# A fifth tile bank and a timetable for block work in layer 1, with shared banks, two projection banks and stepwise finishing in layer 2, of a two-layer relational graph convolution

## The chip, the cores and the metric

The kernel runs on one core of one Trainium2 chip. The metric is the device time of one execution in microseconds. The median of three runs of the kernel before is 3691.99 us (3690.94 to 3702.55).

## The reference

There are N = 12500 nodes with C = 128 features, E = 200000 edges sorted by destination, and ten relations. The relation of an edge is the position of the largest of ten columns of its attributes. Two layers of relational convolution are followed by a residual and a layer norm:

```
def _rgcn_layer(x, src, dst, edge_type, w_rel, root, bias):
    seg  = dst * 10 + edge_type
    sums = segment_sum(x[src], seg, N * 10)
    cnt  = segment_sum(1, seg, N * 10)
    mean = (sums / max(cnt, 1)).reshape(N, 10, C)
    return einsum('nrd,rdo->no', mean, w_rel) + x @ root + bias
h   = relu(layer(x, ..., w_rel1, root1, b1))
out = layernorm(x + layer(h, ..., w_rel2, root2, b2))
```

## The kernel before

**Tiles and blocks.** Edges are worked on in 1563 tiles of 128. For each tile GpSimd (POOL in the profile) issues one indirect DMA, the gather (L833), that brings 128 source rows into a buffer `g`; VectorE (DVE) makes one-hot columns `oh` that say to which node and relation an edge goes, scaled by 1/count (L840); TensorE (PE) multiplies the two, which sums the edges of each node and relation into a PSUM bank; DVE adds the bank into accumulators in SBUF. Nodes are taken in blocks of 256, and a block is complete about every 32 tiles. All of it is in one program order that is written out by hand: three small queues of closures (`todo`, `between`, `jobs`) say at which tile a step is issued. Each engine takes its instructions in that order, so an instruction that waits holds up everything that is behind it on its engine.

**Layer 1.** The first 177 gathers bring rows of `x` (512 B); the other 1386 bring rows of a table XH that holds x and, for nodes that are done, h (1 KB), so that their product is at once a part of layer 2's sum. The products (L1077) go to four PSUM banks `zp`, two tiles in each; DVE adds them (L866) eight tiles later (BEHIND is 2 parts of 4 tiles). POOL may be 16 tiles ahead: four buffers of four tiles, each free when its last product is done.

When a block is complete, `finish(k, t)` issues: ten products with the relations' weights and one with root (L826, L828) into a `pf` bank, ScalarE (ACT) writes h, transposed, as `a` (L745); two transposes (L951) and an ACT copy `hb` (L958) give rows, which go to XH; and h times layer 2's ten relation weights goes out as the table YD. These are six matmuls per block (L934), four tiles apart, all into the one bank `yb`, and each is followed by an ACT copy `ys` (L940) and a store, which `kept_rows` issues when the next one comes. SD is the store of layer 2's sums so far, `cleared` zeroes accumulators on ACT (L795), and `turn` and `turned` transpose the next block's x (L996, L1003). The eight banks are: two `pf`, in which `projected`, the transposes, `turn` and the preparation of later tiles (`jobs`) take turns, one in which counts are kept, `yb`, and four `zp`.

**Layer 2.** Edges whose source had no h when layer 1 came by are gathered now from YD: 177 plain tiles (idxE) and then 678 "second" tiles (idxB), which are sorted by source class into bunches of 4, 2 or 1 tiles that accumulate into one window of 12 to 119 columns. Each bunch takes a bank of its own: three `zy`, and two more `zq` in the second part. POOL may be some 40 tiles ahead. `seen` brings in the blocks' stored sums SD: ten matmuls (L1521) into the one bank `alone`, every 12 tiles, with a DVE add (L1528) nine tiles after the first. `finish(j)` ends a block: two PE transposes (L1540), and at once behind them the layer norm on DVE and ACT (L773 to L783) and the store.

Of the kernel before, what the change touches and what calls it, by code (L numbers as in the profile page):

```python
# [9 lines left out]
F32 = mybir.dt.float32  # L10
# [3 lines left out]
ALU = mybir.AluOpType  # L14
# [6 lines left out]
P = 128  # L21
# [28 lines left out]
HB = 4  # L50
SPLIT = 64
LEAD = 40
LAST = 40
READY = 5
NEAR = 4
GAPW = 112
LOW = 1 << 13
# [11 lines left out]
def rgcn_resnorm_kernel(ctx: ExitStack, tc: tile.TileContext, x, src, dst, attr, w_rel1, root1, b1,  # L69
# [428 lines left out]

    def weights_in():
        for l, (wr, ro, bi) in enumerate(((w_rel1, root1, b1), (w_rel2, root2, b2))):  # L500
            t = const.tile([P, NREL, C], F32, name=f"w{l}")
# [238 lines left out]
    def shifted(po, k, l):  # L740

        n = block(k)[1]
        tail = {NBLK - 1: "e", NBLK - 2: "d"}.get(k, "")
        a = fin.tile([P, P if tail else 3 * P], F32, name="a" + tail)
        nc.scalar.activation(a[:, :n], po[:, :n], AF.Identity if l else AF.Relu, bias=bsb[l])  # L745
        return a
# [159 lines left out]
    def layer_1():  # L906
# [6 lines left out]
        def finish(k, t):  # L913
# [12 lines left out]
            assert not reused or t + 7 * u <= (starts[k] + RN - OFF - WN) // STEP  # L926

            fin_a[k] = shifted(po.pop(), k, 0)

            def projected_rows(b, h, r):  # L930
                kept_rows()
                m = min(HB, NREL - r) * C
                yb = yb_ if u else next_of("zp", fixed)
                nc.tensor.matmul(yb[:h, :m], fin_a[k][:, b * P:b * P + h], wsb[1][:, r:r + m // C, :], start=True, stop=True)  # L934
                unkept.append(lambda: projected_kept(yb, b, h, r))

# [51 lines left out]
            if k + 1 < NBLK - 1:  # L988
# [17 lines left out]
                todo.at(t + w * u, turn)  # L1006
                todo.at(t + (w + 1) * u, turned_kept)

        unkept = []

        def kept_rows(_=None):
# [407 lines left out]
    def layer_2():  # L1419
# [39 lines left out]
            return min(lo for lo, _ in r), max(hi for _, hi in r) + w  # L1459

        reaches = [reach(b) for b in bunches]
        cuts = list(range(0, N, BN)) + [a for a in range(0, N, P) if abs(a - edge) < BN]
        cuts = sorted(set(cuts))
        ranges.append([(a, b - a) for a, b in zip(cuts, cuts[1:] + [N])])
# [37 lines left out]

        def rows_in_turn(j):
            if j < NB2:
                xbs[finals[j]] = next_of("x", xs)
                rows_dma(xbs[finals[j]], x, finals[j], False)

        def seen_in(j):
# [6 lines left out]
        def seen(j, i):  # L1515
            k = heavy[j]
            n0, n, _ = block(k)
            po = alone[0]

            def one(r):  # L1520
                nc.tensor.matmul(po[:, :n], wsb[1][:, r, :], sds[k][:, r, :n], start=(r == 0), stop=(r == NREL - 1))  # L1521
                if r == NREL - 1:
                    sds.pop(k)
                    seen_in(j + 2)

            def added(_):
                assert k in begin[:begins]
                nc.vector.tensor_tensor(acc2[:, n0:n0 + n], acc2[:, n0:n0 + n], po[:, :n], op=ALU.add)  # L1528
                whole.add(k)
            for r in range(NREL):  # L1530
                between.at(i + 2 * r // 3, lambda _, r=r: one(r))
            between.at(i + 9, added)

        def finish(j):
            k = finals[j]
            n0, n, subs = block(k)
            assert k in whole or k not in heavy
            pr = ps_f.tile([P, 4, C], F32, name="pf")
            for b, h in subs:
                nc.tensor.transpose(pr[:h, b, :], acc2[:, n0 + b * P:n0 + b * P + h], ident)  # L1540
            normed(k, xbs.pop(k), pr, (next_of("v", vs), next_of("o", os_)))
            rows_in_turn(j + 3)

        rowP = comp.tile([1, 2 * CT], I32, name="rowP")
        for c in range(2):
# [20 lines left out]
        for p in range(-AH, NB + BE):  # L1566
            if p == plain - AH:
                assert wanted[0] in ready
                masking.close()
                ps_n = fast.enter_context(tc.tile_pool(name="ps_n", bufs=1, space=PSUM))  # L1570
                banks[:] = [next_of("zp", banks) for _ in banks] + [ps_n.tile([P, YB], F32, name=f"zq{j}") for j in range(2)]
# [16 lines left out]
            if p < NB:  # L1588
                second, t0, n, w = bunches[p]
                oh = ohs.pop(p)  # L1590
                zps[p] = zp = next_of("zp", banks)
# [12 lines left out]
                for j in range(n):  # L1604
                    g, at = gs.pop(j)
                    o = 0 if second else j * w
                    nc.tensor.matmul(zp[:, o:o + w], g[:, at * C:(at + 1) * C], oh[:, j * w:(j + 1) * w],  # L1607
                                     start=not second or j == 0, stop=not second or j == n - 1)
                    between.run(issued[p] + j + 1)
                i = issued[p + 1]  # L1610
# [7 lines left out]
            if opened is None and wanted[0] in ready:  # L1618
                opened = i
                for j in range(2):  # L1620
                    seen_in(j)
            for q in [q for q in sorted(zps) if q <= p - (1 if p >= NB - 4 else BE)]:
                second, t0, n, w = bunches[q]
                for j in range(1 if second else n):
                    t = t0 + j
                    if (second, t) not in offs:
# [10 lines left out]
                    nc.vector.tensor_tensor(s, s, zps[q][:, j * w:(j + 1) * w], op=ALU.add)  # L1637
                del zps[q]
            todo.run(i)
            summed_to = min(zps, default=min(p + 1, NB))  # L1640
            while ended < NB2 and done_at[finals[ended]] <= summed_to and (finals[ended] in whole or finals[ended] not in heavy):
                finish(ended)
# [172 lines left out]
```

## Time and profile before

| | us |
|---|---|
| median of three runs | 3691.99 (3690.94 to 3702.55) |
| the profiled execution | 3655.59, of which the span of instructions is 3653.8 |
| PE busy | 2254.1 (62%) |
| PE loading weights | 1859.4 (51%) |
| DVE busy | 1994.0 (55%) |
| ACT busy | 514.6 (14%) |
| POOL busy, 2418 gathers | 2294.6 (63%) |

No engine is busy for more than two thirds of the span. Four stages follow each other, and each is a run of gathers: 177 of x, 1386 of XH, 177 of YD by idxE, 678 of YD by idxB. A row of the groups of instructions reads: line, engine, operation, out<-in, count, then busy time and the mean ns of one, and behind the second bar how long the engine stood idle just before these instructions, and what ended most of it. In a row of the waits the three numbers are the total in us, how often, and the longest. "issue" is time in which the profile shows nothing that was waited for, "remote" is a release by something that the profile cannot name.

### The profile page before, as it was taken

Reading aid. Unit: us, or ns where it says so; the run is one execution under the profiler, and the core shown is the slowest. Engines: PE = TensorE matmul, PEld = TensorE weight load, DVE = VectorE, ACT = ScalarE, POOL = GpSimd, SP = SyncE. Lnnn points to the kernel's source line nnn. Section 1 sums busy time; section 2 is a strip of 40 time slices with the busy share of each in tenths; the row PEclk is TensorE's granted clock in tenths of the full one; section 3 lists DMA queues with packets and bytes.
Section 4 is the critical chain, followed back from the end, with each engine's and each line's share of the span. In section 5 each row is a group of like instructions: output and inputs, shape, how many; then the busy total and the mean of one; then the engine's idle time right before and its main releaser. Section 6 shows DMA issues by size and latency. Waiting matters only on the chain. (4 is left out here: it accounts for less than half of the span.)

```text
span 3653.8 us, 38569 instructions
## 1 busy us (share of the span) xinstructions
PE 2254.1 (62%) x11125; PEld 1859.4 (51%) x11125; DVE 1994.0 (55%) x6434; ACT 514.6 (14%) x799; POOL 2294.6 (63%) x2430
## 2 busy tenths in 40 slices
PE   1556677677676767676667667733556566566534
PEld 0445565565555555555555555623445555555433
DVE  4646576867565757565656565428654333233333
ACT  1111121212121212122212121100000000000000
POOL 5663666666666666666666666566566666666664
PEclk7677877878888888887888877855667777677655
DMA  4553656555555555555656555531144444444322
GB/s 122 154 170 96 189 155 192 153 186 165 172 172 169 172 177 176 171 182 158 191 159 194 158 161 157 146 98 51 46 117 135 143 137 140 136 151 135 97 61 51
DMA packets 376423, 529.31 MB, mean 145 GB/s; under 512 B 55904, under 2 KB 283707, under 8 KB 376204
## 3 DMA queue, kind: packets, MB, share of 16 engines
q0 software_dynamic: 99552, 249.45, 23.9%
q1 hardware_dynamic: 249209, 264.48, 22.4%
q10 hardware_dynamic: 27443, 12.82, 1.2%
q8 instruction: 93, 1.52, 0.2%
q14 instruction: 126, 1.03, 0.1%
HBM read 372.75 MB, written 160.19 MB: 146 GB/s over the span
## 5 line engine op out<-in xcount | busy, mean ns | idle before, releaser
L833 POOL DMA_INDIRECT g<-XH,idxE x1386 | 1314.1, 948 | 737.7 <-issue 364.8
L1077 PEld LDWEIGHTS zp<-oh,g 128*128 128x128 f32 x5898 | 901.7, 229 | 407.3 <-DVE cc L866 201.5
L1077 PE MATMUL zp<-oh,g 128*128 128x120 f32 x5898 | 943.1, 317 | 247.3 <-DVE cc L866 159.0
L866 DVE TENSOR_TENSOR cc<-cc,zp 128x240 f32 (+1 forms) x1563 | 607.1, 388 | 787.1 <-remote 353.0
L833 POOL DMA_INDIRECT g<-YD,idxB x678 | 642.6, 948 | 339.8 <-issue 185.9
L934 PE MATMUL yb<-w,a 128*128 128x512 f32 (+1 forms) x576 | 345.2, 689 | 346.0 <-ACT ys L940 183.1
L840 DVE TENSOR_SCALAR oh<-bank,keyE,wE 128x120 f32<-128x120 f32 x1563 | 517.7, 394 | 0.0
L1521 PE MATMUL alone<-cc,w 128*128 128x256 f32 (+2 forms) x920 | 339.4, 485 | 136.4 <-DVE cc L1528 72.8
L1607 PEld LDWEIGHTS zy<-oh,g 128*128 128x128 f32 x1168 | 245.9, 273 | 222.5 <-DVE cc L1637 155.1
L1607 PE MATMUL zy<-oh,g 128*128 128x12 f32 (+30 forms) x1168 | 237.2, 330 | 197.3 <-DVE cc L1637 148.2
L940 ACT ACTIVATE ys<-yb 128x512 f32<-128x512 f32 (+2 forms) x291 | 153.0, 526 | 1334.4 <-remote 553.7
L934 PEld LDWEIGHTS yb<-w,a 128*128 128x128 f32 x576 | 110.8, 240 | 379.1 <-ACT ys L940 203.6
L1521 PEld LDWEIGHTS alone<-cc,w 128*128 128x128 f32 x920 | 195.3, 247 | 158.3 <-DVE cc L1528 76.5
L826 PE MATMUL pf<-cc,w 128*128 128x256 f32 (+2 forms) x1040 | 248.4, 396 | 15.1 <-issue 9.2
L833 POOL DMA_INDIRECT g<-in_x_dram,idxE x177 | 167.8, 948 | 135.7 <-PE zp L1077 59.3
L833 POOL DMA_INDIRECT g<-YD,idxE x177 | 168.6, 953 | 111.1 <-issue 60.6
L826 PEld LDWEIGHTS pf<-cc,w 128*128 128x128 f32 x1040 | 205.7, 212 | 49.3 <-issue 19.8
L795 ACT ACTIVATE cc<-zero 128x1280 f32<-128x1280 f32 x170 | 214.6, 1262 | 0.0
L840 DVE TENSOR_SCALAR oh<-columns,keyB,wB 128x45 f32<-128x45 f32 (+35 forms) x678 | 177.0, 336 | 0.2 <-issue 0.2
L1637 DVE TENSOR_TENSOR cc<-cc,zy 128x12 f32 (+24 forms) x306 | 58.9, 192 | 177.8 <-remote 145.5
L1607 PEld LDWEIGHTS zq<-oh,g 128*128 128x128 f32 x542 | 113.2, 258 | 30.8 <-issue 18.4
L1528 DVE TENSOR_TENSOR cc<-cc,alone 128x256 f32<-128x256 f32 (+2 forms) x46 | 18.6, 405 | 199.3 <-remote 159.0
(265 smaller groups left out, 1563.5 us busy)
## 6 DMA issues: line engine op xcount, KB each, us to landing
SD<-cc SPq DMA_DIRECT2D x41, 1280.0 KB
cc<-SD SPq DMA_DIRECT2D x41, 1280.0 KB
YD<-ys SPq DMA_DIRECT2D x194, 256.0 KB
m<-in_edge_attr_dram SPq DMA_DIRECT2D x48, 672.0 KB
g<-XH,idxE POOLq DMA_INDIRECT x1386
YD<-ys SPq DMA_DIRECT2D x97, 128.0 KB
XH<-hb SPq DMA_DIRECT2D x44, 256.0 KB
g<-YD,idxB POOLq DMA_INDIRECT x678
```

Of the source, the lines that this page charges most:

```text
L795: nc.scalar.activation(cc[:, l, h * H:(h + 1) * H, o:o + n], zero[:, None, :n].to_broadcast([P, H, n]), AF.Copy)
L826: nc.tensor.matmul(po[:, :n], wsb[l][:, r, :], sums[:, r], start=(r == 0), stop=(w is None and r == NREL - 1))
L833: nc.gpsimd.indirect_dma_start(out=g[:, j * C:(j + n) * C], out_offset=None, in_=table, in_offset=bass.IndirectOffsetOnAxis(ap=idx, axis=0))
L840: nc.vector.tensor_scalar(oh[:, j * m:(j + 1) * m], cols[:, :m], keys[:, j:j + 1], weights[:, j:j + 1], op0=ALU.is_equal, op1=ALU.mult)
L866: nc.vector.tensor_tensor(s, s, z, op=ALU.add)
L934: nc.tensor.matmul(yb[:h, :m], fin_a[k][:, b * P:b * P + h], wsb[1][:, r:r + m // C, :], start=True, stop=True)
L940: nc.scalar.activation(ys[:h, :m], yb[:h, :m], AF.Copy)
L1077: nc.tensor.matmul(zp[:, o + l * KW:o + (l + 1) * KW], g[:, (slot[j] + l) * C:(slot[j] + l + 1) * C], oh[:, j * KW:(j + 1) * KW], start=Tr ...
L1521: nc.tensor.matmul(po[:, :n], wsb[1][:, r, :], sds[k][:, r, :n], start=(r == 0), stop=(r == NREL - 1))
L1528: nc.vector.tensor_tensor(acc2[:, n0:n0 + n], acc2[:, n0:n0 + n], po[:, :n], op=ALU.add)
L1607: nc.tensor.matmul(zp[:, o:o + w], g[:, at * C:(at + 1) * C], oh[:, j * w:(j + 1) * w], start=not second or j == 0, stop=not second or j = ...
L1637: nc.vector.tensor_tensor(s, s, zps[q][:, j * w:(j + 1) * w], op=ALU.add)
```

## The change

**Layer 1.** `zp` has five banks instead of four; `yb` is gone. For blocks up to K1 (44 of them) `finish` calls a new function `spread`, a timetable of steps at fixed numbers of tiles after the block is complete. The six projection matmuls become `unit`s that take a `pf` bank each, and each copy with its store (`unit_out`) is issued two tiles later, always ahead of the next unit. The identity is kept as an eleventh slot behind layer 2's weights, so that the last unit of a 128-row half (relations 8 and 9) is one matmul of 384 columns that also gives the transposed rows; the two transposes (L951) of a block are gone, and `hb` is copied in two halves. In the last blocks one `zp` bank takes the place of `yb`. READY goes from 5 to 7: rows of h may be read from XH eight tiles later than before, which moves seven gathers more to the second part of layer 2 (2425 in all).

**Layer 2.** Bunches share banks: a bank takes up to eight tiles or 512 columns. Second-part banks are three `zy` and one `zq`; `alone` has two banks in turn, and its add comes 20 tiles after the first matmul instead of nine. Sums are taken two banks behind. `finish` is three steps: transposes at least 8 tiles later, `measured` (sum, statistics, ACT's root) 9 tiles behind, `scaled` 4 behind that; in the last 32 tiles (RUSH) they follow at once.

On PE in the middle of layer 1, before: the matmuls into `yb` (L934) with products (L1077) between; DMASW is a gather's arrival, DVE the sum that empties a bank, Activation a copy on ACT.

```order
1593 L934 MATMUL yb<-w_391,a 128x512
1594 L1077 MATMUL zp_409<-oh_97,g_87 128x120 [waits DMASW4_49,DVE_49]
...
1599 L1077 MATMUL zp_410<-oh_97,g_87 128x120 [waits DMASW6_49,DVE_49]
...
1603 L934 MATMUL yb<-w_391,a 128x512 [waits Activation_49]
1604 L1077 MATMUL zp_407<-oh_98,g_88 128x120 [waits DMASW0_49,DVE_49]
...
1608 L1077 MATMUL zp_408<-oh_98,g_88 128x120 [waits DMASW2_49,DVE_49]
...
1612 L934 MATMUL yb<-w_391,a 128x256 [waits Activation_49]
```

The same place after the change, also on PE (L1033 are the units, L1145 the products, L1052 is `turn`, and L297 belongs to the jobs).

```order
1554 L1033 MATMUL pf<-w_113,a 128x384 [waits Activation_49]
1555 L1145 MATMUL zp_407<-oh_96,g_86 128x120 [waits DMASW2_49,DVE_49]
...
1559 L1033 MATMUL pf<-w_113,a 128x384
1560 L1145 MATMUL zp_408<-oh_97,g_87 128x120 [waits DMASW4_49,DVE_49]
...
1564 L297 MATMUL pf<-w_113,s_f 128x128 [waits DVE_49,PE_49,Activation_49]
1565 L1145 MATMUL zp_409<-oh_97,g_87 128x120 [waits DMASW6_49]
...
1573 L1052 MATMUL pf<-w_113,hb_6654 128x128 [waits DMAHW1_49,PE_49,Activation_49]
...
1583 L1033 MATMUL pf<-w_113,a 128x512 [waits Activation_49]
```

Every `yb` matmul waited for ACT's copy of the one before it; the units stand in a rotation of two banks with the other users of `pf`, and most of them (218 of 264 over the program) still carry a wait for ACT.

On PE in the second part of layer 2, before: each bunch goes to the next bank (`zy`, `zq`), and the first matmul of a block's ten waits for DVE's add of the block before.

```order
4712 L1607 MATMUL zq_17204<-oh_93,g_87 128x46 [waits DMASW3_49,DVE_49]
...
4719 L1499 MATMUL pf<-cc,root_393 128x256 [waits DMAHW2_49,Activation_49]
4720 L1607 MATMUL zy_15678<-oh_94,g_87 128x67 [waits DMASW7_49,DVE_49]
...
4722 L1607 MATMUL zy_15679<-oh_95,g_87 128x67 [waits DMASW1_49,DVE_49]
...
4724 L1607 MATMUL zy_15680<-oh_96,g_88 128x46 [waits DMASW3_49,DVE_49]
4725 L1521 MATMUL alone<-cc,w_391 128x256 [waits DMAHW3_49,DVE_49]
```

And after: three bunches (oh_96 to oh_98) share the bank zy_15855 before zy_15856 is taken.

```order
4685 L1737 MATMUL zy_15855<-oh_96,g_90 128x76 [waits DMASW1_49,DVE_49]
...
4687 L1624 MATMUL pf<-w_113,cc 128x128 [waits DVE_49]
...
4689 L1737 MATMUL zy_15855<-oh_97,g_91 128x76 [waits DMASW3_49,DVE_49]
4690 L1600 MATMUL alone_17337<-cc,w_113 128x256 [waits DMAHW6_49,DVE_49]
...
4694 L1737 MATMUL zy_15855<-oh_98,g_91 128x48 [waits DMASW5_49]
...
4702 L1737 MATMUL zy_15856<-oh_92,g_91 128x76 [waits DMASW1_49,DVE_49]
...
4711 L1600 MATMUL alone_17336<-cc,w_113 128x256 [waits DMAHW1_49,DVE_49]
```

The two `alone` banks alternate, so a block's matmuls wait for the add of the block before last; more of the tile products carry a wait for DVE than before (323 instead of 114 over layer 2).

On DVE in the second part, before: the add of `alone` (L1528) stands between the sums (L1637) and one-hots (L840) and waits for PE.

```order
5479 L1637 TENSOR_TENSOR cc<-cc,zq_17203 128x89 [waits DVE_49]
5480 L840 TENSOR_SCALAR oh_94<-columns,keyB,wB 128x93 x4
5481 L1528 TENSOR_TENSOR cc<-cc,alone 128x256 [waits PE_49]
...
5484 L1637 TENSOR_TENSOR cc<-cc,zq_17204 128x89 [waits DVE_49]
5485 L840 TENSOR_SCALAR oh_95<-columns,keyB,wB 128x98 x4
```

And after, where L1660 and L1662 are the step `scaled`, alone between other blocks' work, and the add (L1607) no longer carries a wait for PE of its own.

```order
5482 L1774 TENSOR_TENSOR cc<-cc,zy_15855 128x85 [waits DVE_49]
5483 L1660 RECIPROCAL rstd<-rstd 128x2 [waits Activation_49]
5484 L1662 TENSOR_SCALAR o_15872<-cc,mv,rstd 128x128 [waits DMAHW5_49,DVE_49]
...
5500 L1774 TENSOR_TENSOR cc<-cc,zy_15856 128x89
...
5504 L842 TENSOR_SCALAR oh_97<-columns,keyB,wB 128x98 x4
5505 L1607 TENSOR_TENSOR cc<-cc,alone_17337 128x256
```

An instruction ahead of it on DVE has waited for a later product already, so the add has none left to wait for.

The diff, cut to its core:

```diff
+RUSH = 32
-READY = 5
+READY = 7
-    ident = const.tile([P, P], F32, name="ident")
+    w1_ident = const.tile([P, NREL + 1, C], F32, name="w1")
+    ident = w1_ident[:, NREL, :]
...
@@ layer_1, finish(k, t)
+            if u and k <= K1:
+                spread(k, t, both, reused)
+                return
+            if not spare:
+                fixed[:] = [next_of("zp", fixed) for _ in fixed]
+                turn_of_["zp"] = 0
+                spare.append(fixed.pop(0))
...
-                yb = yb_ if u else next_of("zp", fixed)
+                yb = spare[0] if u else next_of("zp", fixed)
...
+        def spread(k, t, both, reused):
+            def unit(b, r):
+                a = fin_a[k][:, b * P:(b + 1) * P]
+                end = r + HB if r + HB < NREL else NREL + 1
+                held[b, r] = yb = ps_f.tile([P, YB], F32, name="pf")
+                nc.tensor.matmul(yb[:, :(end - r) * C], a, w1_ident[:, r:end, :], start=True, stop=True)
+            def unit_out(b, r):
+                yb = held.pop((b, r))
+                m = min(HB, NREL - r) * C
+                if r + HB >= NREL:
+                    nc.scalar.activation(hbs[k][:, b, C:], yb[:, m:m + C], AF.Copy)
+                ys = next_of("ys", staged)
+                nc.scalar.activation(ys[:, :m], yb[:, :m], AF.Copy)
+                nc.sync.dma_start(by_node[row:row + P, r * C:r * C + m], ys[:, :m])
+            def rows_out():
+                rows_dma(hbs.pop(k), XH[N:], k, True)
+                nc.sync.dma_start(hT[:, n0:n0 + n], fin_a[k][:, :n])
...
+            steps = [(4, sums_out), (6, lambda: unit(0, 8)), (8, lambda: unit_out(0, 8)),
+                     (8, lambda: unit(1, 8)), (10, lambda: unit_out(1, 8)), (10, rows_out)]
...
-        yb_ = ps_z.tile([P, YB], F32, name="yb")
-        fixed = [ps_z.tile([P, YB], F32, name=f"zp{i}") for i in range(4)]
+        fixed = [ps_z.tile([P, YB], F32, name=f"zp{i}") for i in range(5)]
@@ layer_2
+        TOGETHER = 8
+        bank_of, cols, tiles = [], YB, 0
+        for p, (second, _, n, w) in enumerate(bunches):
+            m = w if second else n * w
+            if cols + m > YB or tiles + n > TOGETHER or p in (plain - 3, plain) or p >= NB - 4:
+                bank_of.append((bank_of[-1][0] + 1 if bank_of else 0, 0))
...
-            po = alone[0]
+            po = alone[j % 2]
-            between.at(i + 9, added)
+            between.at(i + 20, added)
...
-        def finish(j):
+        def finish(j, i):
-            pr = ps_f.tile([P, 4, C], F32, name="pf")
-            for b, h in subs:
-                nc.tensor.transpose(pr[:h, b, :], acc2[:, n0 + b * P:n0 + b * P + h], ident)
-            normed(k, xbs.pop(k), pr, (next_of("v", vs), next_of("o", os_)))
+            def turned_rows(i):
...
+                if jobs.due or i >= NG - RUSH:
+                    measured(i)
+                else:
+                    todo.at(i + 9, measured)
...
+            if i >= NG - RUSH:
+                todo.run(END)
+                turned_rows(i)
+            else:
+                at = max(i + 8, free_from[0])
+                free_from[0] = at + 11
+                todo.at(at, turned_rows)
...
-                banks[:] = ... + [ps_n.tile([P, YB], F32, name=f"zq{j}") for j in range(2)]
-                alone.append(ps_n.tile([P, YB], F32, name="alone"))
+                banks[:] = ... + [ps_n.tile([P, YB], F32, name="zq")]
+                alone += [ps_n.tile([P, YB], F32, name=f"alone{j}") for j in range(2)]
...
-            for q in [q for q in sorted(zps) if q <= p - (1 if p >= NB - 4 else BE)]:
+            if p >= NB - 4:
+                due = [q for q in sorted(zps) if q < p]
+            else:
+                due = [q for q in sorted(zps) if bank_of[q][0] <= bank_of[p][0] - 2]
+                if p >= plain:
+                    due = due[:max(2, sum(bank_of[q][0] <= bank_of[p][0] - 3 for q in due))]
```

More of the change, by code (lines that the diff above doesn't have):

```diff
@@ new lines, in measured @@
+            def measured(i):
+                while unscaled:
+                    unscaled[0](i)
+                pr, xb = held.pop("pr"), xbs.pop(k)
+                held["v"] = v = next_of("v", vs)
+                held["mv"] = mv = small.tile([P, 4, 2], F32, name="mv")
+                held["rstd"] = rstd = small.tile([P, 4], F32, name="rstd")
+                for p, s in spans(k):
+                    nc.vector.tensor_tensor(v[:p, s], pr[:p, s], xb[:p, s], op=ALU.add)
+                for b, h in subs:
+                    st = small.tile([P, nc.vector.BN_STATS_DIM], F32, name="st")
+                    nc.vector.bn_stats(st[:h], v[:h, b, :])
+                    nc.vector.bn_aggr(mv[:h, b, :], st[:h])
+                for p, s in spans(k):
+                    nc.scalar.activation(rstd[:p, s], mv[:p, s, 1], AF.Sqrt, bias=eps[:p])
+                rows_in_turn(j + 3)
+                unscaled.append(scaled)
+                if i < NG - RUSH:
+                    todo.at(i + 4, scaled)
+                else:
+                    scaled(i)
@@ new lines, in scaled @@
+            def scaled(_):
+                if scaled not in unscaled:
+                    return
+                unscaled.remove(scaled)
+                v, mv, rstd = (held.pop(a) for a in ("v", "mv", "rstd"))
+                o = next_of("o", os_)
+                for p, s in spans(k):
+                    nc.vector.reciprocal(rstd[:p, s], rstd[:p, s])
+                for b, h in subs:
+                    nc.vector.tensor_scalar(o[:h, b, :], v[:h, b, :], mv[:h, b, 0:1], rstd[:h, b:b + 1],
+                                            op0=ALU.subtract, op1=ALU.mult)
+                rows_dma(o, out, k, True)
@@ L1590, in layer_2 @@
                 oh = ohs.pop(p)
-                zps[p] = zp = next_of("zp", banks)
+                zp, col = zps[p] = (next_of("zp", banks) if not bank_of[p][1] else zps[p - 1][0]), bank_of[p][1]
                 for j in range(n):
```

59 lines of the change are left out of this document (51 added, 8 removed).

## The prediction

> **What bounds the kernel now.** I read the page first, then the groups of instructions on POOL, since no engine is over two thirds busy and gathers run from start to end.
>
> ```profile
> PE   2254.1 (62%) x11125; PEld 1859.4 (51%) x11125; DVE 1994.0 (55%) x6434; ACT 514.6 (14%) x799; POOL 2294.6 (63%) x2430
> L833 POOL DMA_INDIRECT g<-XH,idxE x1386 | 1314.1, 948 | 737.7 <-issue 364.8 <-PE zp L1077 167.7 <-remote 158.9
> L833 POOL DMA_INDIRECT g<-YD,idxB x678 | 642.6, 948 | 339.8 <-issue 185.9 <-remote 97.8 <-PE zy L1607 33.7
> L833 POOL DMA_INDIRECT g<-YD,idxE x177 | 168.6, 953 | 111.1 <-issue 60.6 <-PE zy L1607 31.9 <-remote 10.5
> L833 POOL DMA_INDIRECT g<-in_x_dram,idxE x177 | 167.8, 948 | 135.7 <-PE zp L1077 59.3 <-issue 44.3 <-remote 29.1
> ```
>
> A gather takes 948 ns, and the four rows add up to 2293.1 us of work and 1324.3 us of idle time before: nearly the whole span of 3653.8. Whatever saves time must let POOL stand idle less. How that idle time is made up, the waits of POOL by stage tell: first the 1386 gathers of layer 1 (308 to 2361 us), then layer 2's second part up to 3300, to 3500 and to 3619.
>
> ```profile
> POOL g L833 <- issue: 364.8, 1189, 0.8
> POOL g L833 <- PE zp L1077: 167.7, 71, 7.3
> POOL g L833 <- remote: 158.9, 79, 3.3
> POOL g L833 <- PE pf L951: 8.3, 6, 2.0
> POOL g L833 <- PE yb L934: 7.8, 4, 2.7
> ```
>
> ```profile
> POOL g L833 <- issue: 124.9, 409, 0.5
> POOL g L833 <- remote: 58.5, 21, 3.5
> POOL g L833 <- PE zy L1607: 29.9, 9, 7.0
> POOL g L833 <- PE pf L1540: 9.0, 5, 4.7
> POOL g L833 <- PE zq L1607: 5.0, 2, 3.1
> L833 POOL DMA_INDIRECT g<-YD,idxB x454 | 430.3, 948 | 232.7 <-issue 124.9 <-remote 58.5 <-PE zy L1607 29.9
> ```
>
> ```profile
> POOL g L833 <- issue: 37.8, 124, 0.3
> POOL g L833 <- remote: 26.4, 8, 3.4
> POOL g L833 <- PE zy L1607: 3.5, 2, 3.2
> L833 POOL DMA_INDIRECT g<-YD,idxB x139 | 131.8, 948 | 69.3 <-issue 37.8 <-remote 26.4 <-PE zy L1607 3.5
> ```
>
> ```profile
> POOL g L833 <- remote: 12.8, 3, 4.3
> L833 POOL DMA_INDIRECT g<-YD,idxB x86 | 81.5, 948 | 38.2 <-issue 23.5 <-remote 12.8 <-DMA g<-YD,idxB 1.2
> ```
>
> "issue" is the pause between gathers that follow at once: 364.8/1189 = 0.307 us. So the floor is 0.948 + 0.307 = 1.255 us per gather, and 2418 of them cost 3035 us. The rest is stalls, in which POOL waits for a buffer, that is for PE to be done. Their number gives the gathers per round, and idle time less 0.307 per gather gives the excess of each gather:
>
> - layer 1: 71 + 79 + 6 + 4 = 160 stalls, 8.7 gathers per round; (737.7 − 425.5)/1386 = 0.225 us excess
> - to 3300: 37 stalls, 12.3 per round; (232.7 − 139.4)/454 = 0.206
> - to 3500: 10 stalls, 13.9 per round; (69.3 − 42.7)/139 = 0.192
> - to 3619: 3 stalls, 28.7 per round; (38.2 − 26.4)/86 = 0.137
>
> Longer rounds cost less per gather, but slowly, since the single stall grows (2.1 us in layer 1, 342.7/160, and 4.3 in the last row). In the stage to 3300 the excess comes to 94 us, in layer 1 to 312. Those are what the change can win at most. What makes a round end in layer 1 shows in PE's waits there, and in a stretch of the timeline.
>
> ```profile
> PE yb L934 <- ACT ys L940: 170.7, 61, 11.2
> PE yb L934 <- issue: 136.8, 47, 6.3
> PE zp L1077 <- DVE cc L866: 110.8, 68, 5.2
> PE pf L951 <- ACT a L745: 37.9, 25, 6.1
> ```
>
> ```profile
> 1511.89 1.03 PE L934 MATMUL yb<-w,a 128*128 128x512 f32 x2
> 1521.73 2.08 PE L934 MATMUL yb<-w,a 128*128 128x512 f32 x2 [6.79 <-ACT ys L940]
> 1521.08 0.60 ACT L940 ACTIVATE ys<-yb 128x512 f32<-128x512 f32 x1 [9.51 <-issue]
> 1523.90 0.94 POOL L833 DMA_INDIRECT g<-XH,idxE  x1 [0.30 <-issue]
> 1527.70 0.94 POOL L833 DMA_INDIRECT g<-XH,idxE  x1 [2.86 <-PE zp L1077]
> ```
>
> A `yb` matmul is recorded until 1512.92. ACT, idle for 9.51 us with no cause named, copies it at 1521.08 only; the next `yb` matmul has to wait for that copy, every product behind it too, and at 1524.84 POOL has filled its buffers and stalls. I read it so: what ACT, DVE and POOL wait for is the completion of matmuls, which comes up to 8 us after the recorded end, and a bank that must make the round trip PE, ACT, PE stops PE for that long.
>
> The Trainium skill, "Perfetto Trace Analysis", section "Tensor Engine Instruction (MATMUL, LD_WEIGHTS)", says that the end of a matmul is an estimate from its size, and that its semaphore follows only once PSUM has acknowledged. The trace agrees in kind (1512.92 against 1521.08); that page has no figure for the delay.
>
> **The change part by part.**
>
> *Layer 1, `yb` and the fifth bank.* PE's four waits above make 456 us; that is more than POOL's excess (312), so a part is covered already by the 16 tiles that POOL is ahead. The one-bank round trip at each of six matmuls goes; instead a unit shares two `pf` banks with `projected`, `turn` and the jobs, whose preparation holds one of the two for some 40 of every 128 tiles (read from the code). The unit's copy is issued two tiles (2.5 us at the floor) after it and the next unit four tiles after, except at the pair of tiles 6 and 8. Against a completion that comes up to 8 us late this is a relief, not a cure. The fifth `zp` bank lets PE run ten tiles instead of eight past the last sum. No gain at all would be 0, and a complete one, down to the last row's 0.137, −(0.225 − 0.137) × 1386 = −122. I take rounds like those of layer 2's stretch between the two middle rows, 0.200, because products there stand in five banks, as they now do in layer 1: −0.025 × 1386 = **−35**.
>
> *The transposes.* The row of L951 is small in work and large in waiting:
>
> ```profile
> L951 PE MATMUL pf<-ident,a 128*128 128x128 f32 x88 | 20.7, 321 | 60.9 <-ACT a L745 53.6 <-DMA g<-XH,idxE 5.4 <-issue 1.9
> ```
>
> They go; the 384-column unit needs the same `a` but six tiles later, not at once, and its cost lies between those of 256 and 512 columns. The wait is one of the four above and is in that −35. On ACT a second `hb` copy per block and the clears (L795) ahead of a copy lie in idle time: ACT is 14% busy. Stores, SD and hT move later on SP's queue by 2 to 10 tiles; nobody in layer 1 waits for them except reads of XH, and READY moves with them. **0**; bounds −5 and +5.
>
> *Seven gathers more.* Their tiles are still gathered in layer 1, for x, so these are added: 7 × (1.255 + 0.16) = **+10**.
>
> *Layer 2, plain part.* Its excess is 111.1 − 177 × 0.307 = 57 us; one wait for a product is among its longest. Three banks now hold 24 tiles instead of 12. DVE is busy there with preparing the second part, which stays, so between 0 and −35 (to 0.137 each, −33) I take **−10**.
>
> *Layer 2, second part.* Here one engine's wait blocks the next:
>
> ```profile
> L1521 PE MATMUL alone<-cc,w 128*128 128x256 f32 (+2 forms) x920 | 339.4, 485 | 136.4 <-DVE cc L1528 72.8 <-issue 60.6 <-DVE oh L840 3.0
> L1528 DVE TENSOR_TENSOR cc<-cc,alone 128x256 f32<-128x256 f32 (+2 forms) x46 | 18.6, 405 | 199.3 <-remote 159.0
> L1540 PE MATMUL pf<-ident,cc 128*128 128x128 f32 x98 | 34.3, 385 | 145.3 <-DVE cc L1637 67.1 <-issue 54.6 <-DVE cc L1528 10.7
> PE zy L1607 <- DVE cc L1637: 40.5, 8, 20.4
> ```
>
> DVE stands 199 us in front of the add of `alone`, with sums and one-hots behind it, and PE stands 136 us in front of the next block's ten, with products behind them. Two banks and an add 20 tiles later break this circle; shared banks let a round take up to 32 tiles in place of 20; the transposes come eight tiles after the last sum. Against it, there are only four banks instead of five, and 323 products (114 before) carry a wait for DVE. The bounds are 0 and the last row's excess everywhere, −(0.069 × 454 + 0.055 × 139) = −39. Nearer to the long rounds, at 0.16, it is −(0.046 × 454 + 0.032 × 139) = **−25**. The end stays: in the last 32 tiles blocks are finished at once as before (bounds −10 and +10).
>
> Sum: −35 + 10 − 10 − 25 = −60 us. The profiled execution took 3655.59 us and would take 3596. It lies 36 us under the median 3691.99, for which I forecast 3632.
>
> **The rivals.** A difference under 0.3%, 11 us, can't be told from none here.
>
> *It converts fully (0.22).* If PE is the pace and not the rounds, the waits count as they stand. 312 us of POOL's excess for 456 of PE's waits is 0.68 per us. Losing 70% of the three rows at `yb` and L951 (345 us) gives −165, and with layer 2 as above (−35) and the gathers (+10) −190: 3502. For it: PE hardly waits for a gather (7.2 of 346.0 us in the row of L934 below). Against it: from 3500 on PE has little to do, and the excess is still 0.137.
>
> ```profile
> 3500.00:3654.00 154.00, 55.64 (x239) 50.45 (x238) 51.35 (x225) 3.84 (x13) 81.49 (x86) 0.50 0.21 53
> ```
>
> The first number behind the length of that stretch is PE's busy time.
>
> *More banks bring nothing (0.13).* Rounds are set by the completions alone; only +10 is left: 3702. For it: rounds of 8.7 and of 13.9 differ by 0.033 us per gather only.
> The Trainium skill, "TensorE: Matmul & The Clock Gate", section "HAM oscillation — how this bites in real kernels", tells of a matmul kernel where doubling the PSUM buffers gave no further gain (125.5 against 126.6 us). No run here shows that yet; the waits at `yb` speak against it.
>
> *The units queue up in `pf` (0.17), slower.* The place is layer 1's two `pf` banks.
>
> ```profile
> L934 PE MATMUL yb<-w,a 128*128 128x512 f32 (+1 forms) x576 | 345.2, 689 | 346.0 <-ACT ys L940 183.1 <-issue 153.6 <-DMA g<-XH,idxE 7.2
> ```
>
> A projection waited 346.0/288 = 1.2 us (each is recorded as two). Now 264 units, some 50 `projected`, 50 `turn` and 80 uses by jobs, about 440, share two banks, one of them often held. Waits of PE go from 346 + 61 (L951) = 407 to 440 × w. The point is w = 0.93 us; at w = 1.2 they grow by 121, which is +82 at 0.68, and with −35 in layer 2 and +10 the time is 3749. For it: 218 of 264 units still wait for ACT; against it: between most units lie four tiles and a copy.
>
> **How the numbers follow.** The forecast itself has 0.48, with a range of its own of 3585 to 3680. Faster takes it and the full conversion, 0.48 + 0.22 = 0.70; the same is the third case, 0.13; slower is the fourth, 0.17. The range from 3500 to 3712 takes in the first three and leaves out the slow case and the far tail of the full conversion.
>
> **What would show it.** In the profile after, layer 1's gathers should have fewer than 130 stalls (over 10.5 per round) and their excess be near 0.20; the waits of units for ACT be under 150 us in place of 307; L951 be gone. In layer 2 the add of `alone` should wait for less than 50 us in place of 199, and gathers by idxB run 15 or more per round. If the units wait over 400 us, the fourth case is it; if POOL's stalls in layer 1 stay at 150 or more with PE's waits gone, the third; if layer 1 takes under 1.40 us per gather, the second. The prediction is also wrong if layer 2's shared banks make the tile products wait for DVE much more than the 40.5 us of now.

## The result, and the profile after

The median is 3779.42 us (3767.46 to 3785.05) against 3691.53: a ratio of 1.0233, 95% interval 1.0214 to 1.0252. The change costs 2.3%, where 1.6% less was forecast.

One fact has to stand first. The times of this kernel have two levels that go by the measurement, not by the kernel: in four of seven measurements the median of the kernel before was 3654 to 3692 us, as in the profile above, and in three it was 3070 to 3073. One chip showed both. Each ratio here compares a kernel with the one before within one measurement, and the level is named: long or short. Two ratios of different measurements can be compared only with care.

The two profiled spans differ by 129 us, more than the medians, since the profiled execution of before lay 36 us under its median. So a part of the differences by stage below is that fast execution. POOL's rows after (busy and idle add up to the time of a stage):

```profile
L835 POOL DMA_INDIRECT g<-XH,idxE x1386 | 1310.7, 946 | 833.9 <-issue 372.7 <-PE zp L1145 239.6 <-remote 157.4
L835 POOL DMA_INDIRECT g<-YD,idxB x685 | 647.5, 945 | 365.9 <-issue 197.4 <-remote 73.5 <-PE zy L1737 61.6
L835 POOL DMA_INDIRECT g<-YD,idxE x177 | 168.7, 953 | 114.9 <-issue 60.3 <-PE zy L1737 32.2 <-remote 15.8
```

Layer 1's 1386 gathers take 2144.6 us in place of 2051.8 (+93, but +70 against the run with layer 2's part alone, shown below, in which the old layer 1 took 2074.5), the second part of layer 2 1013.4 in place of 982.4 (+31, of which seven gathers more are 10), the plain part +4. POOL's waits in layer 1 after the change:

```profile
POOL g L835 <- PE zp L1145: 239.6, 70, 11.1
POOL g L835 <- remote: 157.4, 68, 3.0
POOL g L835 <- PE pf L1033: 8.6, 5, 2.7
POOL g L835 <- DVE cc L868: 23.1, 11, 3.6
```

By the rows that the prediction counted (PE and remote) that is 143 stalls of 2.84 us in place of 160 of 2.14, or 9.7 gathers per round in place of 8.7. But now DVE ends some of the pauses too. Counted as all pauses of POOL over 0.6 us in this stage, there are 160 in place of 164, of 2.86 us in place of 2.21. So the rounds hardly grew; the single pause did. PE's and DVE's groups:

```profile
L1145 PE MATMUL zp<-oh,g 128*128 128x120 f32 x5898 | 939.5, 311 | 393.5 <-issue 274.2 <-DVE cc L868 81.4 <-DVE ty L520 9.0
L1033 PE MATMUL pf<-w,a 128*128 128x512 f32 (+1 forms) x528 | 332.7, 719 | 182.1 <-ACT ys L1041 115.5 <-issue 35.0 <-ACT fT L1057 14.8
L828 PE MATMUL pf<-cc,w 128*128 128x256 f32 (+2 forms) x1040 | 272.8, 428 | 53.1 <-issue 20.5 <-ACT ys L1041 17.1 <-DVE cc L868 8.4
L1600 PE MATMUL alone<-cc,w 128*128 128x256 f32 (+2 forms) x920 | 349.8, 484 | 98.9 <-issue 95.5 <-DVE cc L1607 2.0
L842 DVE TENSOR_SCALAR oh<-columns,keyB,wB 128x45 f32<-128x45 f32 (+37 forms) x685 | 178.3, 330 | 191.6 <-remote 102.3 <-PE zy L1737 49.0 <-PE alone L1600 25.9
L1607 DVE TENSOR_TENSOR cc<-cc,alone 128x256 f32<-128x256 f32 (+2 forms) x46 | 18.4, 399 | 14.4 <-remote 14.4
```

The waits that the change was to take away are gone: the projections' 346 us are 182, and the 199 us of DVE ahead of the add of `alone` are 14. They stand elsewhere now: the products (L1145) wait 393 us in place of 247, most of it for nothing that the profile names, `projected` (L828) 53 in place of 15, and DVE's one-hots in layer 2 192 in place of 0.2. The timelines of PE's weight loads and of its matmuls show what the unnamed wait looks like. In this stretch POOL issues gathers without a pause up to 1534.62:

```profile
1529.84 0.19 PEld L1145 LDWEIGHTS zp<-oh,g 128*128 128x128 f32 x1 [0.82 <-issue]
1531.28 0.19 PEld L1145 LDWEIGHTS zp<-oh,g 128*128 128x128 f32 x1 [1.25 <-issue]
1532.71 0.19 PEld L1145 LDWEIGHTS zp<-oh,g 128*128 128x128 f32 x1 [1.24 <-issue]
```

```profile
1530.55 0.26 PE L1145 MATMUL zp<-oh,g 128*128 128x120 f32 x1 [1.19 <-issue]
1531.99 0.26 PE L1145 MATMUL zp<-oh,g 128*128 128x120 f32 x1 [1.18 <-issue]
1533.41 0.26 PE L1145 MATMUL zp<-oh,g 128*128 128x120 f32 x1 [1.15 <-issue]
1536.98 1.41 PE L1145 MATMUL zp<-oh,g 128*128 128x120 f32 x5 [0.36 <-issue]
```

Loads and matmuls take turns, and one starts every 0.70 to 0.73 us, until POOL pauses; then five matmuls take 1.41 us. I call it that PE is held up. Counted over the traces, three or more entries in a row that start 0.68 to 0.75 us apart occur 54 times in this one (154 us together), 15 times in the one before (39 us), and never in the nine traces at the short level. The two levels of the changed kernel differ by 703 us, so these stretches mark the long level but are a small part of what it costs.

### The profile page after: what moved, and what is told of

It reads as the page before. It is cut to its first block, busy times and chain, and to the rows that moved or that the text cites. A ratio compares the mean times of both kernels' runs of the same rounds, so it can differ in the third digit from the quotient of the medians.

```text
span 3783.2 us, 38678 instructions
## 1 busy us (share of the span) xinstructions
PE 2307.9 (61%) x11051; PEld 1856.3 (49%) x11051; DVE 1998.1 (53%) x6443; ACT 513.7 (14%) x843; POOL 2295.7 (61%) x2437
## 3 DMA queue, kind: packets, MB, share of 16 engines
q0 software_dynamic: 99776, 249.91, 23.5%
## 5 line engine op out<-in xcount | busy, mean ns | idle before, releaser
L835 POOL DMA_INDIRECT g<-XH,idxE x1386 | 1310.7, 946 | 833.9 <-issue 372.7
L1145 PE MATMUL zp<-oh,g 128*128 128x120 f32 x5898 | 939.5, 311 | 393.5 <-issue 274.2
L1145 PEld LDWEIGHTS zp<-oh,g 128*128 128x128 f32 x5898 | 880.9, 223 | 573.0 <-issue 377.1
L1033 PE MATMUL pf<-w,a 128*128 128x512 f32 (+1 forms) x528 | 332.7, 719 | 182.1 <-ACT ys L1041 115.5
L1737 PE MATMUL zy<-oh,g 128*128 128x12 f32 (+30 forms) x1380 | 282.4, 326 | 235.4 <-issue 135.6
L1737 PEld LDWEIGHTS zy<-oh,g 128*128 128x128 f32 x1380 | 293.6, 271 | 264.4 <-issue 144.2
L828 PE MATMUL pf<-cc,w 128*128 128x256 f32 (+2 forms) x1040 | 272.8, 428 | 53.1 <-issue 20.5
L828 PEld LDWEIGHTS pf<-cc,w 128*128 128x128 f32 x1040 | 225.2, 230 | 121.1 <-issue 46.1
L842 DVE TENSOR_SCALAR oh<-columns,keyB,wB 128x45 f32<-128x45 f32 (+37 forms) x685 | 178.3, 330 | 191.6 <-remote 102.3
L1041 ACT ACTIVATE ys<-pf 128x512 f32<-128x512 f32 (+1 forms) x264 | 138.2, 523 | 780.5 <-remote 427.2
L1033 PEld LDWEIGHTS pf<-w,a 128*128 128x128 f32 x528 | 100.9, 238 | 196.2 <-ACT ys L1041 128.3
L1774 DVE TENSOR_TENSOR cc<-cc,zy 128x12 f32 (+21 forms) x342 | 65.3, 197 | 247.0 <-remote 133.8
L1579 ACT ACTIVATE cc<-pf,b 128x256 f32<-128x256 f32 (+2 forms) x51 | 23.7, 465 | 690.5 <-remote 338.5
L1737 PEld LDWEIGHTS zq<-oh,g 128*128 128x128 f32 x344 | 74.1, 262 | 62.8 <-issue 51.6
```

The lines of the kernel that those rows point to most:

```text
L828: nc.tensor.matmul(po[:, :n], wsb[l][:, r, :], sums[:, r], start=(r == 0), stop=(w is None and r == NREL - 1))
L835: nc.gpsimd.indirect_dma_start(out=g[:, j * C:(j + n) * C], out_offset=None, in_=table, in_offset=bass.IndirectOffsetOnAxis(ap=idx, axis=0))
L842: nc.vector.tensor_scalar(oh[:, j * m:(j + 1) * m], cols[:, :m], keys[:, j:j + 1], weights[:, j:j + 1], op0=ALU.is_equal, op1=ALU.mult)
L1033: nc.tensor.matmul(yb[:, :(end - r) * C], a, w1_ident[:, r:end, :], start=True, stop=True)
L1041: nc.scalar.activation(ys[:, :m], yb[:, :m], AF.Copy)
L1145: nc.tensor.matmul(zp[:, o + l * KW:o + (l + 1) * KW], g[:, (slot[j] + l) * C:(slot[j] + l + 1) * C], oh[:, j * KW:(j + 1) * KW], start=Tr ...
```

## The experiments

| kernel | long level | short level |
|---|---|---|
| the change | 1.0233 (1.0214 to 1.0252) | 1.0013 (1.0003 to 1.0024) |
| layer 1's part | 1.0185 (1.0146 to 1.0224) | |
| layer 2's part | 1.0014 (1.0004 to 1.0023) | |
| the change, four tile banks | 1.0186 (1.0139 to 1.0232) | |
| six gather buffers on before | 1.0020 (1.0010 to 1.0030) | |
| units in a bank of their own | 1.0088 (1.0058 to 1.0118) | 1.0017, 1.0011 |
| units in pf, old times | 1.0593 (1.0563 to 1.0623) | 0.9997, 0.9990 |
| units half and half | 1.0175 (1.0149 to 1.0201) | |
| the same, last unit not in pf | | 1.0021 (1.0012 to 1.0030) |
| 347 products twice, on before | 1.0021 (1.0004 to 1.0039) | 1.0001 |
| a memset per gather, on before | 1.0260 (1.0223 to 1.0298) | 1.0517, 1.0521 |

**Which layer.** Layer 1's hunks of the diff with READY alone, and layer 2's alone.

> Layer 1's part of the change alone (five tile banks, timetable, READY 7), layer 2 as before. In the two traces layer 1's XH gathers take 90 us longer after the change and layer 2's second part 30 us. Theory A (the matmuls' completions come in bursts once the gathers pause; the number of rounds is set by POOL's four-tile buffers, and the timetable only lengthens the pauses): +75 to +95 us, XH stage near 2140 us, again some 160 stalls of 2.9 us. Theory B (the parts disturb each other, for instance READY's seven gathers or shifted stores): under +50 us.

> Layer 2's part alone, layer 1 and READY as before. Theory A: the second part's stalls grow by 0.3 us each as in the trace after (+13 us), without the seven gathers: +5 to +25 us. Theory B (layer 2's loss is only the seven gathers more and a layer 1 that ends badly): 0 +- 8 us.

Layer 1's part costs 61 us of medians (3748.4 against 3687.6; 54 to 83 by the ratio's interval), between the two theories; layer 2's costs 7, which both theories allow. So most of the loss is layer 1's, and layer 2's expected 35 us are simply absent. The two parts make 68 us; the whole change cost 88 in another measurement, and the difference is open. Groups of DVE and of POOL in the kernel with layer 2's part:

```profile
L1540 DVE TENSOR_TENSOR cc<-cc,alone 128x256 f32<-128x256 f32 (+2 forms) x46 | 18.4, 400 | 14.3 <-remote 14.3
L841 DVE TENSOR_SCALAR oh<-columns,keyB,wB 128x45 f32<-128x45 f32 (+35 forms) x678 | 177.9, 333 | 201.5 <-remote 116.7 <-issue 28.3 <-PE zy L1670 27.3
```

```profile
L834 POOL DMA_INDIRECT g<-YD,idxB x678 | 641.9, 947 | 350.3 <-issue 187.6 <-remote 74.5 <-PE zy L1670 40.1
L834 POOL DMA_INDIRECT g<-XH,idxE x1386 | 1313.9, 948 | 760.6 <-issue 368.5 <-PE zp L1078 186.3 <-remote 154.1
```

DVE waits about as long as before (215.8 us in these two rows against 199.5), ahead of the one-hots instead of the add; POOL's idle time is 350 in place of 340. I read it so that the wait was for completions of matmuls and moved to the next instruction that needs one. The last row is layer 1 as it was before the change: 2074.5 us.

**The fifth bank, and the lookahead.**

```diff
-        fixed = [... for i in range(5)]
+        fixed = [... for i in range(4)]
```

> The kernel after with four tile banks in layer 1 instead of five (the fifth bank is only used by the last blocks). Theory A (rounds go in steps of four tiles, ten tiles of banks are worth eight): within 15 us of the kernel after, that is +75 to +100 us against before. Theory C (five banks help, and the loss is all from the units in pf): slower than the kernel after by 30 us or more, +120 against before.

```diff
-NEAR = 4
+NEAR = 6
```

> The kernel before with six gather buffers instead of four in layer 1 (POOL may be 24 tiles ahead, READY 7 so that rows of h are stored in time; seven gathers more in layer 2, +10 us). Theory A: rounds grow from 8.6 to 12 or more, XH stage from 1.48 to about 1.44 us per gather: -40 to -60 us, with the gathers -30 to -50. Theory D (PE's own waits at yb and at zp set the pace, whatever the lookahead): within 12 us of before, or +10 for the gathers.

With four banks the change costs 69 us of medians, 6 less than theory A's range and far from theory C's 120. It is no slower than with five, so the fifth bank buys no time here. What it does is move a wait. The products with four banks:

```profile
L1145 PE MATMUL zp<-oh,g 128*128 128x120 f32 x5898 | 942.1, 314 | 496.0 <-DVE cc L868 293.3 <-issue 175.0 <-DVE oh L842 9.6
```

With five they wait 81 us in place of 293 for DVE's sums, and 274 in place of 175 for nothing that is named. More lookahead buys nothing either (+0.2%, about the seven gathers that READY 7 adds). Its pauses are not fewer (177 over 0.6 us in layer 1, against 164 before), so my theory that POOL's buffers cut the rounds falls.

**Where the units go.** Units in one bank of their own with the timetable's times, and units in `pf` at the old times. Two measurements of each came to the short level, where neither could show:

> The kernel after with four tile banks, and the timetable's units in one bank of their own, as yb was, instead of in the two pf banks. Theory E (sharing pf with projected, turn and the jobs is what costs layer 1): recovers most of the loss, that is within 25 us of layer 2's part alone (3695). Theory F (the times of the timetable cost it, whatever the bank): stays at 3740 to 3770, as with the units in pf (3757).

> The kernel after with four tile banks, units in pf, but every step of a finished block at the tile at which it stood before the change (units at 8, 12, 16, 20, 24, 28, each copy right before the next unit; clears at 8, 12, 20, 24; turn at 20). Theory F: recovers most, 3690 to 3715. Theory E: stays at 3740 to 3770.

> The changed kernel itself, on whatever chip this call gets. The first eight runs came from two chips: on one before takes 3688 us, with the same pauses in POOL as in the two traces shown; on the other it takes 3073 us, gathers follow each other without a stall and no PE queue entry takes 0.70 us. Where before takes some 3690 us: +2.0 to +2.6%, as first measured. Where it takes some 3070 us, POOL's floor sets the time: seven gathers more, +9 us, that is +0.1 to +0.4%.

At the short level POOL follows its floor, and the waits vanish by themselves. Groups of POOL and of PE in the changed kernel there:

```profile
L835 POOL DMA_INDIRECT g<-XH,idxE x1386 | 1313.9, 948 | 437.8 <-issue 371.0 <-PE zp L1145 34.5 <-DMA g<-XH,idxE 11.0
```

```profile
L1145 PE MATMUL zp<-oh,g 128*128 128x120 f32 x5898 | 925.4, 304 | 373.7 <-DMA g<-XH,idxE 211.3 <-DVE cc L868 141.3 <-DVE oh L842 9.3
L1033 PE MATMUL pf<-w,a 128*128 128x512 f32 (+1 forms) x528 | 300.1, 655 | 1.3 <-ACT fT L1057 0.7 <-ACT ys L1041 0.6
```

The same program waits 1.3 us ahead of the units, not 182, and its products wait most for gathers. So the banks alone do not make these waits; they come with the long level. The rest is +5 us of medians (1 to 7 by the interval). Seven gathers at 1.255 us would be 9, but the kernel with the old times has the same seven and costs nothing here (0.9997, 0.9990), so what the +5 is stays open. The two kernels with moved units at the long level:

> Where before takes some 3690 us: theory E within +0.8% of before; theory F +1.4 to +2.2%; theory I +0.7 to +1.6%. Where before takes some 3070 us: +0.1 to +0.2%.

> Where before takes some 3690 us: theory F (the timetable's times cost layer 1) within +0.7% of before; theory E (sharing pf costs it) +1.4 to +2.2%; theory I (neither alone) +0.7 to +1.6%. Where before takes some 3070 us: 0 +- 0.2%.

Groups of PE in the one with a bank of its own, then with units in `pf` and four tile banks, then with units in `pf` at the old times:

```profile
L1033 PE MATMUL yb<-w,a 128*128 128x512 f32 (+1 forms) x528 | 345.7, 745 | 244.5 <-ACT ys L1041 169.1 <-issue 49.2 <-DVE cc L868 14.4
L828 PE MATMUL pf<-cc,w 128*128 128x256 f32 (+2 forms) x1040 | 237.9, 386 | 8.0 <-issue 5.6 <-PE yb L1033 1.0 <-DVE cc L868 0.9
```

```profile
L1033 PE MATMUL pf<-w,a 128*128 128x512 f32 (+1 forms) x528 | 342.6, 739 | 171.4 <-ACT ys L1041 99.0 <-issue 64.0 <-DVE cc L868 5.3
L828 PE MATMUL pf<-cc,w 128*128 128x256 f32 (+2 forms) x1040 | 257.9, 410 | 50.8 <-issue 21.2 <-ACT ys L1041 17.6 <-DVE cc L868 10.9
```

```profile
L1033 PE MATMUL pf<-w,a 128*128 128x512 f32 (+1 forms) x528 | 337.1, 725 | 199.3 <-ACT ys L1041 126.6 <-issue 39.4 <-remote 17.9
L828 PE MATMUL pf<-cc,w 128*128 128x256 f32 (+2 forms) x1040 | 289.3, 442 | 185.5 <-ACT ys L1041 130.8 <-issue 48.7 <-DVE cc L868 3.9
```

Moving the units out of `pf` halves the loss (1.0186 to 1.0088, in two measurements) although the units themselves then wait longer (244 us against 171). The 0.9% that is left lies just outside theory E and in theory I; layer 2's part (0.1%) and the seven gathers explain some of it, the rest is open.

In `pf` at the old times the loss is 5.9%, which no theory allowed. So with the units in `pf` the timetable is far better than the old times; with a bank of their own no run shows that it helps. The run is also not quite the old order: rows of h, which were stored at tile 4 before the change, are stored at tile 16 in it (10 in the timetable), and POOL waits for those stores. A row of POOL's waits in layer 1, and its group:

```profile
POOL g L835 <- DMA XH<-hb: 46.8, 7, 8.2
L835 POOL DMA_INDIRECT g<-XH,idxE x1386 | 1310.2, 945 | 939.3 <-issue 373.8 <-PE zp L1145 206.3 <-DVE cc L868 108.4
```

In these three the wait of `projected` rises with the time: 8, 51 and 186 us. To see whether the units' own waits count at all, three of a block's six went to each kind of bank:

```diff
-                held[b, r] = yb = yb_
+                held[b, r] = yb = ps_f.tile([P, YB], F32, name="pf") if b else yb_
```

> The kernel after with four tile banks, three of a block's six units in a bank of their own and three in pf. Where before takes some 3650 to 3690 us, theory E (each turn of a bank between PE and ACT can cost a pause; what counts is how many banks the turns have): not slower than the units all in a bank of their own (+0.9%), 0 to +0.9%. Theory J (any use of pf by the units hurts projected and turn): between that and the units all in pf, +1.1 to +1.9%. Where before takes some 3070 us: +0.1 to +0.2%.

```profile
L828 PE MATMUL pf<-cc,w 128*128 128x256 f32 (+2 forms) x1040 | 279.5, 431 | 123.9 <-ACT ys L1041 67.8 <-issue 47.8 <-DVE cc L868 5.7
L1033 PE MATMUL yb<-w,a 128*128 128x512 f32 (+1 forms) x264 | 171.6, 740 | 6.1 <-DVE cc L868 3.8 <-issue 2.3
L1033 PE MATMUL pf<-w,a 128*128 128x512 f32 (+1 forms) x264 | 153.0, 664 | 3.0 <-issue 2.3 <-DVE wp L636 0.5
L1146 PE MATMUL zp<-oh,g 128*128 128x120 f32 x5898 | 974.9, 318 | 554.3 <-DVE cc L868 303.1 <-issue 220.0 <-DVE oh L842 6.8
```

The units wait 9 us in all, in place of 346 before, and the kernel is 1.75% slower than before: theory E falls, J holds. So taking the waits at `yb` away wins nothing by itself. The wait of `projected` does not order the times either: it is 124 us here and 51 with all six units in `pf`, at the same loss (1.0175 and 1.0186). One more run was to take away only the unit right ahead of `projected`:

> The kernel of the mixed banks, but the last unit of a block (tile 30, right ahead of the next block's projected) goes to the bank of its own: four units there, two in pf. Where before takes some 3650 to 3690 us, theory K (what costs is the wait of projected for the copy of a unit just ahead of it; in the mixed kernel that wait is 124 us, in the one with all units in a bank of their own 8): the wait falls under 30 us and the time to +0.9% or less. Theory J (any use of pf by units): stays at +1.4 to +1.9%. Where before takes some 3070 us: +0.1 to +0.2%.

It came to the short level, so whether that one wait carries the loss is not shown.

**Whose time counts.** More work on PE, and more on POOL, both on the kernel before:

```diff
-                    for l in (0, 1) if i >= NX else (0,):
+                    for l in ((0, 0, 1) if j == 0 else (0, 1)) if i >= NX else (0,):
```

> The kernel before with one of eight products in layer 1 done twice (the first one's result is overwritten): 347 more matmuls of 120 columns without a wait of their own, at 0.32 us of PE time each 111 us. Theory G: +60 to +160 us. Theory H: under +30 us, since PE has 38% idle.

> The kernel before with 347 products more in layer 1 that wait for nothing of their own. On the other chip they cost nothing (0.0%). Where before takes some 3690 us: theory G (PE, held up while gathers run, is what POOL waits for): +60 to +200 us; theory H: under +30 us.

```diff
+        nc.gpsimd.memset(g[:1, j * C:j * C + 1], 0.0)
         nc.gpsimd.indirect_dma_start(out=g[:, j * C:(j + n) * C], ...
```

> The kernel before with a memset of one element on POOL ahead of each gather, some 0.1 to 0.3 us each, 240 to 700 us of POOL time over 2418 gathers. Theory G (PE paces the kernel, POOL's stalls only absorb that): under a third of the added POOL time shows, the stalls shrink. Theory H (rounds of gathers plus a fixed drain pace it): nearly all of the added time shows.

> A memset on POOL ahead of each gather; where before takes 3073 us it cost +158 us, all of its time. Where before takes some 3650 to 3690 us: theory G (POOL's pauses only absorb): under +50 us; theory H (PE's completions come only in pauses of the gathers, so that a round's gathers and its pause add up): +110 to +160 us.

(At the short level the first cost nothing, and the second +158 us of medians, that is 0.065 us per gather.) At the long level 347 matmuls cost 6 us of medians, 0.02 each, so PE's working time is not the price either, and theory G falls. The memset costs 2.6%, 90 us of medians or some six tenths of what it costs at the short level: neither theory's value. So POOL's pauses take up a part of added time and let the larger part through. The row of the memset shows that part: the waits for buffers now stand ahead of it, 420 us, where all of POOL's idle time but "issue" was some 670 before.

```profile
L833 POOL MEMSET g<- 1x1 f32 x2418 | 219.1, 91 | 420.3 <-remote 217.8 <-PE zp L1078 138.8 <-PE zy L1608 28.8
```

## Why the prediction was wrong

**Layer 1, −35: measured +61 for its part alone.** The step that failed is the table of rounds, from which the term −35 was taken. It read the four stages as one curve on which longer rounds cost less per gather. In layer 1 the rounds hardly changed, and the excess went from 0.225 (0.242 in the run with layer 2's part alone) to (833.9 − 425.5)/1386 = 0.295 us instead of down to 0.200. With the units in `pf` at the old times there are only 131 pauses over 0.6 us, so the longest rounds of all (10.6 gathers), and yet the excess is the largest: 0.371, or 0.337 without the 46.8 us of waits for stores of h. So longer rounds did not make the gathers cheaper, and what the change altered was the single pause, which got longer. What made it longer is shown in part: with the units out of `pf` half of the loss is gone, and with three of six in `pf` it is all there. How a shared bank does that, and what the other half is, stays open.

**The waits as a price.** I held 456 us of PE's waits in layer 1 to be what makes rounds end. Half and half took the units' waits to 9 us with a loss of 1.75%. The idle time did not go away; it turned up at the products, which waited 247 us before, 496 with all units in `pf` and four tile banks, and 554 half and half. I read it so that a wait in front of a held-up engine is only where its lateness becomes visible.

**The slow rival** had the right place, `pf`, and 0.17. Its mechanism was wrong: units were to wait over 400 us and wait 182. Others in the rotation wait more than they did (`projected` 15 to 53, `turn` 0 to 30, the jobs 110 to 144), but that is 102 us more against 225 fewer at the units and the transposes (407 to 182), so these waits fell in all. Of the signs that I gave beforehand several of the forecast's own came true while the time rose: units wait 115 us for ACT (under 150), L951 is gone, the add of `alone` waits 14 us (under 50), gathers by idxB run 15.6 per round by the rows counted then. They were signs of the edit, not of the time. 143 stalls lie between two of the cases.

**The Trainium skill's remark** on doubled PSUM buffers in one matmul kernel ("TensorE: Matmul & The Clock Gate", "HAM oscillation — how this bites in real kernels") was no further gain. For the fifth bank the runs here agree: 1.0186 without it, 1.0233 with it, in two measurements. It was the third case of the forecast, "more banks bring nothing"; that case alone would have given +10 us and leaves out the loss from `pf`.

**Layer 2, −10 and −25: measured +7 for the part.** The waits that were named did go (199 to 14 us on DVE, 73 to 2 for DVE at `alone`); POOL's idle time did not. The feared wait of the tile products for DVE did not come: in the `zy` rows it fell from 148 to 73 us. The mistake is the same: the wait is found again at the next instruction.

**Seven gathers, +10:** no run has them alone. Six gather buffers on before, which adds the same seven, cost 8 us at the long level; at the short level the kernels that have them cost between −3 and +6 us. The size is not contradicted, and not shown.

**Not doubted at all:** that the level itself could vary. A trace with POOL idle in pauses of 2 to 4 us against a floor of 1.255 us per gather had the question in it: 3035 us of gathers, and at the short level the kernel takes 3070.

## What to carry to other kernels

When an engine waits for a bank, look first whether the other side is late: compare the recorded end of the matmul with the time at which its consumer starts. If the completion is late, more banks or fewer waits can just move the idle time to the next instruction, as they did here in both layers. Be wary of taking a bank of its own away from a long round trip between two engines: here the units in the shared `pf` cost about 1% more than in a bank of their own. That the step which starts the next block (`projected`) is what suffers was not shown. And time a change again on another occasion before believing a price read from one trace.

## What the runs showed of the hardware

While POOL issues gathers back to back at the long level, PE can advance by one queue entry in 0.70 to 0.73 us, whether it is a load of weights or a matmul; at the short level, with the same gathers (948 ns each), no three entries in a row do so in nine traces. What holds PE up is open. One chip showed both levels within an hour. The gathers take the same time at both, and so do the packets of their DMA queue, as the pages of the changed kernel at the long and at the short level say:

```profile
q0 software_dynamic: 99776, 249.91, 23.5%
q0 software_dynamic: 99776, 249.91, 28.5%
```

23.5% of 3783.2 us is 889, 28.5% of 3082.1 is 878. So the transfers are not slower at the long level. The granted clock of PE does differ, 0.740 against 0.817 on average; no run shows whether that is a cause of the long level or follows from PE's idling more. The change costs 0.13% or 2.3% by the level, and no kernel tried here beats the one before at the long level.
